# Layer 0's first weight product as seven block products, with every engine's order written out

## The chip, the cores and the metric

The kernel runs on one core of one Trainium2 chip. The metric is device time in microseconds (us), from the first to the last instruction of the core. The core has a matrix engine (PE; its weight loads are listed apart as PEld), a vector engine (DVE), an activation engine (ACT), a general engine (POOL, also called GpSimd) and a queue that only issues transfers (SP). [...]

## What is computed

Four graph layers run one after the other on x of 128 x 64 x 256 numbers (128 graphs, 64 nodes, 256 channels), all in fp32. The change touches only the first half of layer 0. Cut to what matters:

```python
h = jnp.maximum(_layernorm(x, axis=-1), 0.0)
x = x + _L0_gnn_ref(h, adj, W1, b1, g1, be1, W2, b2, g2, be2)

def _L0_gnn_ref(features, A, W1, b1, g1, be1, W2, b2, g2, be2):
    ...
    agg = jnp.einsum('nm,bmd->bnd', A_hat, features)
    x = agg.reshape(-1, d)
    h = jax.nn.relu(_batchnorm(x @ W1.T + b1, g1, be1))
    out = h @ W2.T + b2
    out = _batchnorm(out, g2, be2)
    return out.reshape(b, n, -1)
```

The batch norm takes its mean and variance over all 8192 rows (graphs times nodes). So no row of `h` can be made before the last row of `x @ W1.T` is there. Layer 1 (two graph products and four small LSTMs), layer 2 (attention) and layer 3 (attention with four heads) follow; they take about 1650 us of the time and are not touched.

## The kernel before

The 8192 rows are cut into 16 chunks of 512 rows (`CH = 512`, `NCH = 16`). A chunk is loaded as a tile of 128 partitions by 4 token tiles by 256 channels (`xt`, three buffers). Layer 0's first half does this for each chunk:

- `ln_stats` takes mean and variance of each token tile on DVE (`bn_stats`, line 159, and `bn_aggr`, line 160), then POOL computes one over the root (`rsqrt`, lines 99 and 100) and, in `ln_apply`, minus mean times that (lines 182 and 183). ACT applies both with a relu, one instruction for each of the four token tiles (line 187), which gives `h` (two buffers).
- `aggregate0` multiplies by the normalised adjacency, two graphs in one 128 x 128 block-diagonal matrix, and turns tokens by channels into channels by tokens on the way (`aggregate`, line 214). Each fp32 product counts as two instructions in the trace, so this is 64 small ones a chunk. The result lies in two PSUM banks; one is copied to the tile `agg` (two buffers) by DVE (line 354) and one by ACT (line 356).
- `product1` multiplies by W1: four blocks of 128 output channels, each over two blocks of 128 input channels, 512 columns wide (line 369; 16 instructions a chunk in the trace). ACT takes each block from PSUM and adds the bias b1 (line 371), and DVE takes its statistics for the batch norm (line 372). The results, `z1`, stay in SBUF for all 16 chunks: blocks 0 and 1 in a tile `z1a`, blocks 2 and 3 in a tile `z1b`.

After the last chunk `bn_params` makes scale and shift for each block of 128 channels from the statistics of all chunks (line 295 on DVE, 99 and 100 on POOL, 299 to 301 on DVE). `relu2` applies them to chunks 0 and 1 on ACT (line 376), and `product2` multiplies these two chunks by W2 (line 385), block by block as they come.

The second product of chunks 2 to 14 is made in another way already: the class `Seven2` takes the 2 x 2 blocks of a product and makes them with seven block products and sums of blocks (Winograd's form of Strassen's method). Its left sums of weights are `w2_sums` (line 508), its right sums are made by `differences` (lines 308 to 311), and its products (line 432) are 256 columns wide, 28 instructions a chunk. A PSUM bank named X collects products 1, 6, 7 and 4 one after the other and is read after each; Y collects 5 and 3; Z holds 2. The four right sums of a chunk lie in one tile of the tag `h1`, which has two buffers.

What sets the order: inside `manual_schedule(engines=...)` an engine named there takes its instructions in the order of the program; engines not named are ordered by a planner. Chunk 0 is written out for all engines, chunks 1 to 15 and `bn_params` for PE alone, `Seven2` for PE, DVE, ACT and POOL. Between these stretches stands `tc.no_sync_barrier()`, a boundary in the order of the instructions that makes no engine wait for another. [...]

## Time and profile before

| | |
|---|---|
| median of 3 runs | 1911.15 us (1910.53 to 1912.87) |
| span of the profiled execution | 1908.6 us |
| the same execution, as timed | 1910.73 us |
| PE busy | 1887.0 us of 1908.6 (99%) |
| DVE, ACT, POOL busy | 1190.7, 979.5, 444.6 us |
| layer 0's first half: chunk 2's aggregation to the first `product2` | 22.34 to 144.37 us |
| in these 122.03 us: PE, DVE, ACT, POOL busy | 121.72, 72.06, 74.65, 25.93 us |
| `Seven2`, steady part (182.49 to 230.80): PE, DVE, ACT, POOL busy of 48.31 us | 48.31, 42.89, 35.58, 39.07 us |

A line of the timeline gives the start and the length of a merged group in us, the engine, the line of the program, the operation, the tile written and read, shapes, and how many instructions were merged; in brackets stands how long the engine had been idle before and what released it. A group of PE instructions is longer than its share of the engine's time[...]: how fast PE goes is read from the distance between starts.

### The profile page before, as it was taken

Reading aid. Unit: us, or ns where it says so; the run is one execution under the profiler, and the core shown is the slowest. Engines: PE = TensorE matmul, PEld = TensorE weight load, DVE = VectorE, ACT = ScalarE, POOL = GpSimd, SP = SyncE. Lnnn points to the kernel's source line nnn. Section 1 sums busy time; section 2 is a strip of 40 time slices with the busy share of each in tenths; the row PEclk is TensorE's granted clock in tenths of the full one; section 3 lists DMA queues with packets and bytes.
Section 4 is the critical chain, followed back from the end, with each engine's and each line's share of the span. In section 5 each row is a group of like instructions: output and inputs, shape, how many; then the busy total and the mean of one; then the engine's idle time right before and its main releaser. Section 6 shows DMA issues by size and latency. Waiting matters only on the chain.

```text
span 1908.6 us, 38821 instructions
## 1 busy us (share of the span) xinstructions
PE 1887.0 (99%) x15137; PEld 1488.3 (78%) x15137; DVE 1190.7 (62%) x3070; ACT 979.5 (51%) x2184; POOL 444.6 (23%) x632
## 2 busy tenths in 40 slices
PE   8999999999999999999999999999999999999998
PEld 5446866886897898799689789879969967777776
DVE  6647844556557656655755764665555567777776
ACT  5657734455456455455544645545554544444453
POOL 4205711211211211121121121112112213232332
PEclk9999999999999999999999999999999999999999
DMA  4113653115424522531632452352144245444433
GB/s 137 60 39 138 223 195 108 49 78 188 132 84 161 182 84 77 189 103 70 215 117 84 161 182 84 103 186 100 54 155 127 92 133 156 134 150 139 144 112 112
DMA packets 110502, 240.39 MB, mean 126 GB/s; under 512 B 11376, under 2 KB 74352, under 8 KB 110320
## 3 DMA queue, kind: packets, MB, share of 16 engines
q1 hardware_dynamic: 109568, 236.57, 37.1%
q8 instruction: 120, 1.97, 0.4%
q0 software_dynamic: 320, 1.05, 0.2%
q14 instruction: 62, 0.51, 0.1%
q10 hardware_dynamic: 432, 0.30, 0.1%
HBM read 169.98 MB, written 67.90 MB: 125 GB/s over the span
## 4 chain that ended last, share of the span: by engine, by line
PE 93%; DVE 4%; ACT 1%; issue 1%; POOL 1%; DMA 0%; SPq 0%; DVEq 0%; ACTq 0%; POOLq 0%
PE x L990 23%; PE g L954 18%; PE z L990 11%; PE y L990 6%; PE v L1264 6%; PE z L369 5%; PE p_q L1271 3%; PE u L743 3%; PE v L729 3%; PE X L1460 3%; PE X L432 2%; PE Y L1460 1%; PE z L385 1%; PE Y L432 1%; PE agg_c L214 1%; PE o L1587 1%
## 5 line engine op out<-in xcount | busy, mean ns | idle before, releaser
L999 DVE TENSOR_TENSOR gates<-gates,x 128x128 f32<-128x128 f32 (+2 forms) x384 | 119.4, 322 | 333.1 <-PE x L990 327.7
L990 PE MATMUL x<-xd,wset 128*128 128x128 f32 (+2 forms) x1280 | 285.0, 310 | 0.1
L990 PE MATMUL x<-hd,wset 128*128 128x128 f32 (+2 forms) x1152 | 246.7, 303 | 0.0
L1048 POOL TENSOR_TENSOR gates<-gates 128x512 f32<-128x512 f32 (+2 forms) x48 | 75.0, 1562 | 647.9 <-ACT gates L882 647.9
L990 PEld LDWEIGHTS x<-xd,wset 128*128 128x128 f32 x1280 | 202.1, 190 | 16.9 <-DVE gates L999 3.1
L882 ACT ACTIVATE gates<-gates,bias 128x256 f32<-128x256 f32 (+4 forms) x384 | 170.4, 490 | 66.4 <-DVE gates L999 63.6
L990 PEld LDWEIGHTS x<-hd,wset 128*128 128x128 f32 x1152 | 185.1, 191 | 5.0
L933 ACT ACTIVATE gates<-g,bias 128x512 f32<-128x512 f32 (+2 forms) x240 | 138.2, 610 | 97.7 <-PE g L954 94.4
L954 PE MATMUL g<-hT,wset 128*128 128x256 f32 (+2 forms) x744 | 184.4, 405 | 1.1 <-DVE hT L893 1.1
L954 PEld LDWEIGHTS g<-hT,wset 128*128 128x128 f32 x744 | 140.5, 190 | 44.1 <-issue 8.8
L954 PE MATMUL g<-hT,wih 128*128 128x512 f32 x384 | 166.4, 592 | 0.0
L996 ACT COPY gates<-y 128x128 f32<-128x128 f32 (+2 forms) x192 | 54.2, 294 | 204.8 <-PE y L990 204.3
L990 PE MATMUL z<-hs,wset 128*128 128x128 f32 (+2 forms) x768 | 154.1, 303 | 0.0
L954 PEld LDWEIGHTS g<-hT,wih 128*128 128x128 f32 x384 | 72.3, 190 | 87.7 <-issue 83.0
L990 PEld LDWEIGHTS z<-hs,wset 128*128 128x128 f32 x768 | 119.8, 191 | 3.3
L369 PE MATMUL z<-agg,w_sb 128*128 128x512 f32 x256 | 114.1, 598 | 0.0
L939 DVE TENSOR_TENSOR cell<-gates 128x512 f32<-128x512 f32 (+2 forms) x80 | 50.5, 650 | 101.6 <-ACT gates L933 101.5
L999 DVE TENSOR_TENSOR gates<-gates,z 128x128 f32<-128x128 f32 (+2 forms) x384 | 104.6, 316 | 0.2
L996 ACT COPY gates<-x 128x128 f32<-128x128 f32 (+2 forms) x192 | 56.5, 296 | 93.7 <-PE x L990 93.0
L882 ACT ACTIVATE gates<-x,bias 128x128 f32<-128x128 f32 (+2 forms) x192 | 74.8, 390 | 50.9 <-PE x L990 48.1
L990 PE MATMUL z<-hT,wset 128*128 128x128 f32 (+1 forms) x512 | 96.9, 301 | 0.0
L369 PEld LDWEIGHTS z<-agg,w_sb 128*128 128x128 f32 x256 | 47.3, 190 | 54.6 <-issue 51.4
(271 smaller groups left out, 3827.0 us busy)
## 6 DMA issues: line engine op xcount, KB each, us to landing
wset<-wfar SPq DMA_DIRECT2D x96, 960.0 KB, 6.4
hT<-far_h SPq DMA_DIRECT2D x124, 128.0 KB, 2.9
far_h<-hm SPq DMA_DIRECT2D x16, 512.0 KB, 3.0
far_n<-xs SPq DMA_DIRECT2D x16, 512.0 KB, 6.9
xs<-far_n SPq DMA_DIRECT2D x64, 128.0 KB, 3.1
far_x<-xs SPq DMA_DIRECT2D x16, 512.0 KB, 3.0
x<-far_x SPq DMA_DIRECT2D x64, 128.0 KB, 3.2
xt<-in_x_dram SPq DMA_DIRECT2D x15, 512.0 KB, 4.0
```

The lines of the kernel that those rows point to most:

```text
L369: nc.tensor.matmul(ps, w1_sb[:, k, m * P : (m + 1) * P], agg[:, k, :], start=(k == 0), stop=(k == KD - 1))
L432: nc.tensor.matmul(self.banks[tag], w, right[:, k, :], start=first and not k, stop=True, skip_group_check=True)
L729: nc.tensor.matmul(banks[m], wg0_sb[:, k, m * P : (m + 1) * P], agg[:, k, :], start=(k == 0), stop=(k == KD - 1))
L882: nc.scalar.activation(gate(q, c, part), src, AF.Tanh if q == 2 else AF.Sigmoid, bias=bs[:, q * KD + c : q * KD + c + 1])
L933: nc.scalar.activation(columns_of(gate(q, c)), natural(banks[q, c][:, :n].rearrange("p (w b) -> p w b", b=nb)), AF.Tanh if q == 2 else AF. ...
L954: nc.tensor.matmul(banks[q, c][:, :n].rearrange("p (w b) -> p w b", b=nb)[:, w, :], block(q, c, k), hv[:, k, w.start * p : (w.stop - 1) * ...
L990: nc.tensor.matmul(folded(self.psum(kind)), wsets[p, self.q][:, BLOCKS[kind][i], :], (ox[self.s] if part == "x" else oh)[kind], start=firs ...
L996: nc.scalar.copy(gate(self.q, kind // 5, halves[kind // 5]), self.psum(kind))
L999: nc.vector.tensor_add(gate(self.q, *dst), gate(self.q, *a), self.psum(kind))
L1048: nc.gpsimd.tensor_mul(gates[:, 0, :, :n], gates[:, 0, :, :n], gates[:, 2, :, :n])
L1264: nc.tensor.matmul(ps[:, i, :], hT[:, k, j, :], w[:, k, first : first + D], start=(k == 0), stop=(k == KD - 1))
L1460: nc.tensor.matmul(st[c, tag][:, i * CH // 2 : (i + 1) * CH // 2].rearrange("p (a n) -> p a n", n=P), w, st[c, "o7"][kind], start=first an ...
```

## The change

Chunks 2 to 14 of `product1` become seven block products too, in a new class `Seven1`. The 2 x 2 blocks are the two 128-channel blocks of `agg` by its two halves of 256 columns. One product is two matrix products of 256 columns (four instructions in the trace), one for each 128 columns of the weight block. The left sums `w1_sums` are made by POOL from `w1_sb`; the four right sums of a chunk are made by POOL into a tile `t1` of tag `h1`. The same tile holds product 2 (`self.z`), which ACT copies out of PSUM and POOL adds to block (0, 0) (`c11`). Blocks are taken from PSUM by four ACT copies and two DVE additions per chunk. Chunks 0, 1 and 15 keep the plain product.

Chunks 1 to 15 are now written out in order for PE, DVE, ACT and POOL. In iteration `c` of the new loop stand the aggregation of chunk `c + 1` (both copies now on ACT), five products of chunk `c` and the last two of chunk `c - 1`, the right sums for `c + 1`, layer-norm statistics of chunk `c + 3`, and layer-norm application of chunk `c + 2`. Loads of x are issued for `c + 4`.

ACT copies `z1` without the bias; `bn_params` is called with `biased=False`, which adds b1 to the mean and then b1 times the scale to the shift, two small DVE instructions for each of the four blocks. `w2_sums` moves from the start of this stretch into iterations 7 to 10. `bn_params` for `bn1` and what follows are now behind a `no_sync_barrier()` of their own.

```diff
@@ -299,6 +300,9 @@
             nc.vector.tensor_mul(sc[:, one], sc[:, one], bn[:, 1, one])
             nc.vector.tensor_mul(sh[:, one], mv[:, m, 0:1], sc[:, one])
             nc.vector.tensor_sub(sh[:, one], bn[:, 2, one], sh[:, one])
+            if not biased:
+                nc.vector.scalar_tensor_tensor(sh[:, one], bn[:, 0, one], sc[:, one], sh[:, one],
+                                               op0=OP.mult, op1=OP.add)
         return sc, sh
...
@@ -336,41 +340,106 @@
     z1, z1whole, h1, hs, aggs = {}, {}, {}, {}, {}
+    xts, shifts = {}, {}
+    halves2 = [slice(0, CH // 2), slice(CH // 2, CH)]
     def load0(c):
-        xt = l0.tile([P, NJ, D], F32, tag="xt", name=f"xt_{c}", bufs=3)
-        nc.sync.dma_start(xt, xr[c])
-        hs[c] = l0.tile([P, NJ, D], F32, tag="h", name=f"h_{c}")
-        return xt
-    def norm0(c):
-        xt = load0(c)
-        ln_apply(hs[c], xt, *ln_stats(xt, f"a{c}"), f"a{c}", by_pool=True)
-    def aggregate0(c):
+        if c < NCH:
+            xts[c] = l0.tile([P, NJ, D], F32, tag="xt", name=f"xt_{c}", bufs=3)
+            nc.sync.dma_start(xts[c], xr[c])
+    def moments0(c):
+        return ln_moments(xts[c], f"a{c}", range(NJ)) if c < NCH else iter(())
+    def shift0(c, late):
+        for mv, rstd in late:
+            nmr = small.tile([P, NJ], F32, tag=f"ln_nmr{NJ}", name=f"nmr_a{c}")
+            nc.gpsimd.tensor_tensor(nmr, mv[:, :, 0], rstd, OP.mult)
+            nc.gpsimd.tensor_scalar(nmr, nmr, -1.0, None, op0=OP.mult)
+            shifts[c] = rstd, nmr
+    def apply0(c, *tiles):
+        if c >= NCH:
+            return
+        if c not in hs:
+            hs[c] = l0.tile([P, NJ, D], F32, tag="h", name=f"h_{c}")
+        rstd, nmr = shifts[c]
+        for j in tiles:
+            nc.scalar.activation(hs[c][:, j, :], xts[c][:, j, :], AF.Relu, bias=nmr[:, j : j + 1],
+                                 scale=rstd[:, j : j + 1])
+    def aggregate0(c, by_both=True):
         aggs[c] = l0.tile([P, KD, CH], F32, tag="agg", name=f"agg_{c}")
         dst = aggs[c].rearrange("p k (j e t) -> p e (k j) t", e=2, t=T)
         for e, ps in enumerate(aggregate(hs.pop(c), ahat_t, f"a{c}")):
-            if e == 0:
+            if by_both and e == 0:
                 nc.vector.tensor_copy(dst[:, e], ps)
             else:
                 nc.scalar.copy(dst[:, e], ps)
-    def product1(c):
-        agg = aggs.pop(c)
+    def new_z1(c):
         lo = res.tile([P, KD, CH], F32, tag=f"r{c}", name=f"z1a_{c}")
         hi = z1b.tile([P, KH - KD, CH], F32, tag=f"z{c}", name=f"z1b_{c}")
         z1[c] = [lo[:, m, :] for m in range(KD)] + [hi[:, m, :] for m in range(KH - KD)]
-        for m in range(KH):
-            if c == 0 and 2 * m == KH:
-                aggregate0(1)
-                ln_apply(hs[2], *third, "a2")
-            ps = bank(f"z1_{c}_{m}")
-            for k in range(KD):
-                nc.tensor.matmul(ps, w1_sb[:, k, m * P : (m + 1) * P], agg[:, k, :],
-                                 start=(k == 0), stop=(k == KD - 1))
-            nc.scalar.activation(z1[c][m], ps, AF.Identity, bias=bn1_sb[:, 0, m : m + 1])
+        z2[c], z1whole[c] = lo, (lo, hi)
+    def stats1(c, *ms):
+        for m in ms:
             nc.vector.bn_stats(st1[:, m, c, :], z1[c][m])
-        z2[c], z1whole[c] = lo, (lo, hi)
+    def block1(c, m, agg):
+        ps = bank(f"z1_{c}_{m}")
+        for k in range(KD):
+            nc.tensor.matmul(ps, w1_sb[:, k, m * P : (m + 1) * P], agg[:, k, :], start=(k == 0),
+                             stop=(k == KD - 1))
+        nc.scalar.copy(z1[c][m], ps)
+    class Seven1:
+        def __init__(self, c):
+            self.c, self.banks = c, {}
+            agg = aggs.pop(c)
+            b = {(k, j): agg[:, k, halves2[j]] for k in range(KD) for j in range(2)}
+            t = l0b.tile([P, KH, CH], F32, tag="h1", name=f"t1_{c}").rearrange("p k n -> p (k n)")
+            n = CH // 2
+            self.z = t[:, 4 * n : 6 * n]
+            t = [t[:, i * n : (i + 1) * n] for i in range(4)]
+            self.sums = differences(nc.gpsimd, t, b[0, 0], b[0, 1], b[1, 0], b[1, 1])
+            self.at = {1: b[0, 0], 2: b[1, 0], 3: b[1, 1], 4: t[3], 5: t[0], 6: t[1], 7: t[2]}
+        def product(self, kind, tag):
+            first = tag not in self.banks
+            if first:
+                self.banks[tag] = bank(f"{tag}1_{self.c}")
+            for i in range(2):
+                if kind in (1, 2, 4):
+                    m, k = {1: (0, 0), 2: (0, 1), 4: (1, 1)}[kind]
+                    w = w1_sb[:, k, (2 * m + i) * P : (2 * m + i + 1) * P]
+                else:
+                    w = w1_sums[:, {5: 0, 6: 1, 7: 2, 3: 3}[kind], i * P : (i + 1) * P]
+                nc.tensor.matmul(self.banks[tag][:, i * CH // 2 : (i + 1) * CH // 2], w, self.at[kind],
+                                 start=first and not i, stop=True, skip_group_check=True)
+        def part(self, m, j):
+            return z1whole[self.c][m][:, :, halves2[j]]
+        def ps(self, tag):
+            return self.banks[tag].rearrange("p (i n) -> p i n", i=2)
+        def copy(self, m, j, tag):
+            nc.scalar.copy(self.part(m, j), self.ps(tag))
+        def add(self, m, j, tag):
+            nc.vector.tensor_add(self.part(m, j), self.part(m, j), self.ps(tag))
+        def c11(self):
+            nc.gpsimd.tensor_tensor(self.part(0, 0), self.part(0, 0),
+                                    self.z.rearrange("p (i n) -> p i n", i=2), OP.add)
...
-        xt = load0(2)
-        third = xt, *ln_stats(xt, "a2")
-        product1(0)
+        load0(2)
+        third = ln_stats(xts[2], "a2")
+        agg = aggs.pop(0)
+        new_z1(0)
+        for m in range(KH):
+            if 2 * m == KH:
+                aggregate0(1)
+                hs[2] = l0.tile([P, NJ, D], F32, tag="h", name="h_2")
+                ln_apply(hs[2], xts[2], *third, "a2")
+            block1(0, m, agg)
+            stats1(0, m)
...
+        w1_sums = l0.tile([P, 4, D], F32, name="w1_sums", bufs=1)
         w2_sums = l0b.tile([P, 4, KH // 2, P], F32, name="w2_sums", bufs=1)
-        a = w2_sb.rearrange("p (i k) (m f) -> p i m k f", i=2, m=KD)
-        for dst, u, v, op in ((0, a[:, 0, 1], a[:, 1, 1], OP.add),
-                              (1, w2_sums[:, 0], a[:, 0, 0], OP.subtract),
-                              (2, a[:, 0, 0], a[:, 0, 1], OP.subtract),
-                              (3, a[:, 1, 0], w2_sums[:, 1], OP.subtract)):
-            nc.gpsimd.tensor_tensor(w2_sums[:, dst], u, v, op)
-        for c in range(1, NCH):
-            if c + 1 < NCH:
-                aggregate0(c + 1)
-            if c + 2 < NCH:
-                norm0(c + 2)
-            product1(c)
-        sc1, sh1 = bn_params(st1, bn1_sb, w0, "bn1", True)
+    tc.no_sync_barrier()
+    def sums_of(dst, a):
+        return [lambda d=d, u=u, v=v, op=op: nc.gpsimd.tensor_tensor(dst[:, d], u, v, op)
+                for d, u, v, op in ((0, a[:, 0, 1], a[:, 1, 1], OP.add),
+                                    (1, dst[:, 0], a[:, 0, 0], OP.subtract),
+                                    (2, a[:, 0, 0], a[:, 0, 1], OP.subtract),
+                                    (3, a[:, 1, 0], dst[:, 1], OP.subtract))]
+    with tc.manual_schedule(engines={mybir.EngineType.PE, mybir.EngineType.DVE,
+                                     mybir.EngineType.Activation, mybir.EngineType.Pool}):
+        load0(3)
+        load0(4)
+        aggregate0(2)
+        late = moments0(3)
+        for _ in range(NJ):
+            next(late)
+        shift0(3, late)
+        for f in sums_of(w1_sums, w1_sb.rearrange("p k (m f) -> p k m f", m=2)):
+            f()
+        late = moments0(4)
+        sevens = {2: Seven1(2)}
+        new_z1(1)
+        agg = aggs.pop(1)
+        load0(5)
+        for m in range(KH):
+            block1(1, m, agg)
+            next(late)
+            stats1(1, m)
+            if m:
+                apply0(3, *((0,), (1,), (2, 3))[m - 1])
+        for f in sevens[2].sums:
+            f()
+        shift0(4, late)
+        more = sums_of(w2_sums, w2_sb.rearrange("p (i k) (m f) -> p i m k f", i=2, m=KD))
+        for c in range(2, NCH - 1):
+            a, z = sevens[c], sevens.get(c - 1)
+            new_z1(c)
+            load0(c + 4)
+            aggregate0(c + 1, False)
+            b = sevens[c + 1] = Seven1(c + 1) if c + 1 < NCH - 1 else None
+            late = moments0(c + 3)
+            a.product(2, "Z")
+            nc.scalar.copy(a.z, a.banks["Z"])
+            next(late, None)
+            next(late, None)
+            apply0(c + 2, 0)
+            if z:
+                z.product(7, "X")
+                z.add(1, 1, "X")
+            if b:
+                for f in b.sums:
+                    f()
+            a.product(1, "X")
+            a.copy(0, 0, "X")
+            a.c11()
+            if z:
+                stats1(c - 1, 0, 1)
+            a.product(5, "Y")
+            a.copy(1, 1, "Y")
+            apply0(c + 2, 1)
+            next(late, None)
+            next(late, None)
+            if z:
+                z.product(4, "X")
+                z.copy(1, 0, "X")
+            apply0(c + 2, 2)
+            shift0(c + 3, late)
+            if c > 6 and more:
+                more.pop(0)()
+            if z:
+                stats1(c - 1, 2, 3)
+            a.product(6, "X")
+            a.copy(0, 1, "X")
+            apply0(c + 2, 3)
+            a.product(3, "Y")
+            a.add(0, 1, "Y")
+        c = NCH - 1
+        new_z1(c)
+        agg = aggs.pop(c)
+        for m in range(KH):
+            if not m:
+                a.product(7, "X")
+                a.add(1, 1, "X")
+                stats1(c - 1, 0, 1)
+            if m == 1:
+                a.product(4, "X")
+                a.copy(1, 0, "X")
+                stats1(c - 1, 2, 3)
+            block1(c, m, agg)
+            stats1(c, m)
+    tc.no_sync_barrier()
+    with tc.manual_schedule(engines={mybir.EngineType.PE}):
+        sc1, sh1 = bn_params(st1, bn1_sb, w0, "bn1", False)
         for c in range(2):
             new_h1(c)
         for k in range(KH):
```

More of the change, by code (lines that the diff above doesn't have):

```diff
@@ L446, in stats @@
             nc.vector.bn_stats(st2[:, m, self.c, :], z2[self.c][:, m, :])
-    halves2 = [slice(0, CH // 2), slice(CH // 2, CH)]
     with tc.manual_schedule(engines={mybir.EngineType.PE, mybir.EngineType.DVE,
@@ L458 @@
             nc.scalar.dma_start(adjt_bd[r, r], adj_t)
-        xts = [l0.tile([P, NJ, D], F32, tag="xt", name=f"xt_{c}", bufs=3) for c in range(2)]
+        for c in range(2):
+            xts[c] = l0.tile([P, NJ, D], F32, tag="xt", name=f"xt_{c}", bufs=3)
         nc.sync.dma_start(xts[0][:, : NJ // 2], xr[0][:, : NJ // 2])
```

## The prediction

> **What bounds the kernel now.** I read the busy shares first, then the windows of the stage that changes, then its timeline.
>
> ```profile
> PE 1887.0 (99%) x15137; PEld 1488.3 (78%) x15137; DVE 1190.7 (62%) x3070; ACT 979.5 (51%) x2184; POOL 444.6 (23%) x632
> ...
> 22.34:144.37 122.03, 121.72 (x1138) 59.25 (x1138) 72.06 (x189) 74.65 (x129) 25.93 (x59) 1.00 0.21 66
> ```
>
> PE has no idle time to speak of, here as elsewhere: between chunk 2's aggregation and the first second product it idles 0.3 of 122 us. So PE instructions removed count in full, and each wait that PE gets is a loss. The timeline gives the price of one chunk, before and in the form that `Seven2` already has:
>
> ```profile
> 47.88 1.16 PE L214 MATMUL agg_a<-ahat_t,h 64*64 64x64 f32 x64
> ...
> 48.97 7.13 PE L369 MATMUL z<-agg,w_sb 128*128 128x512 f32 x16
> ...
> 56.04 1.16 PE L214 MATMUL agg_a<-ahat_t,h 64*64 64x64 f32 x64
> ...
> 182.49 1.03 PE L432 MATMUL Z<-z1b,w_sb 128*128 128x256 f32 x4
> ...
> 188.53 1.03 PE L432 MATMUL Z<-z1b,w_sb 128*128 128x256 f32 x4
> ```
>
> From start to start a chunk takes 56.04 - 47.88 = 8.16 us: 1.09 for the aggregation, 16 x 0.429 = 6.86 for the product, 0.2 at the change between them. Twenty-eight instructions of 256 columns take 188.53 - 182.49 = 6.04 us, 0.863 for a product of four. Three more views bear on what the new order waits for.
>
> ```profile
> 25.17 1.41 POOL L508 TENSOR_TENSOR w_sums<-w_sb 128x256 f32<-128x256 f32 x2 [3.67 <-DMA w_sb<-in_w2t_dram]
> ...
> 28.13 0.23 POOL L99 TENSOR_SCALAR rstd_a<-mv_a 128x4 f32<-128x4 f32 x1
> ...
> 30.14 2.08 ACT L187 ACTIVATE h<-xt,nmr_a,rstd_a 128x256 f32<-128x256 f32 x4 [2.28 <-POOL nmr_a L183]
> ```
>
> POOL: four sums of 256 columns take 28.13 - 25.17 = 2.96 us, and from the start of the root to ACT's first use of the shift there are 2.01 us.
>
> ```profile
> 185.94 1.03 PE L432 MATMUL X<-t,w_sb 128*128 128x256 f32 x4
> ...
> 187.00 0.86 DVE L308 TENSOR_TENSOR t<-z1a 128x512 f32<-128x512 f32 x1 [0.75 <-PE X L432]
> ```
>
> The first right sum of a chunk, which overwrites a part of the tile that only product 5 has read, still waited for product 4 of the chunk before last, 1.06 us after that one's start. A buffer of `h1` comes free only whole.
>
> ```profile
> 23.01 1.29 DVE L372 BATCH_NORM_STATS2 st<-z1b 128x6 f32<-128x512 f32 x2 [2.76 <-ACT z1b L371]
> 24.22 0.27 DVE L144 TENSOR_SCALAR mask<-adj_bd 64x64 f32<-64x64 f32 x2
> ...
> 140.14 0.69 DVE L372 BATCH_NORM_STATS2 st<-z1a 128x6 f32<-128x512 f32 x1 [1.02 <-ACT z1a L371]
> 140.86 0.59 DVE L295 BATCH_NORM_AGGREGATE mv_bn<-st 128x2 f32<-128x96 f32 x1
> ...
> 143.05 1.52 ACT L376 ACTIVATE h<-z1a,sh_bn,sc_bn 128x512 f32<-128x512 f32 x2 [1.23 <-DVE sh_bn L301]
> 143.94 0.19 PEld L385 LDWEIGHTS z<-h,w_sb 128*128 128x128 f32 x1 [0.24 <-ACT h L376]
> ```
>
> Line 144 needs only `adj_bd`, there since 6 us, and DVE idled 2.76 us before line 372; yet it ran after it: nothing passes a `no_sync_barrier`. And today block 0's statistics (line 295) run while PE still multiplies blocks 1 to 3 of chunk 15; that hides the batch norm.
>
> [...] The first 34 `idle_a` transposes took 5.45 us, 33 steps of 0.157, where `idle_b` has steps of (1.47 - 0.27)/11 = 0.109: 1.6 us lost to a cold start. [...] here 128x512 takes 1.27 to 1.78 us on POOL (line 309) and 0.68 at best on DVE.
>
> **The change, part by part.**
>
> *Products.* For 13 chunks 16 x 0.429 = 6.86 becomes 6.04 us: 13 x 0.82 = -10.7 us, all on the path. Weight loads of 190 ns fit into steps of 216.
>
> *One iteration, if PE sets it:* 0.2 + 1.09 + 6.04 = 7.34 us. ACT: seven copies at a step of 0.49 (49.18 to 49.66 at line 356) and four applications at 0.49: 5.4 us. DVE: four tiles of statistics at 0.53, four statistics of 512 at 0.61, two additions at 0.6 (673 ns at line 772): 5.8 us. POOL: sums 2.96, `c11` 1.3 (line 309 at its quickest, 1.27), root and shift 2.0: 6.3 us; with one w2 sum (0.73) 7.0. All are below 7.34, so only order can hurt. ACT's order: a copy starts 1.12 us after its product's start (185.08 to 186.20). From product 5's start there follow 1.12, five ACT steps 2.46, the last application 0.59, the wait 0.06, the aggregation of that tile 0.4, products 2, 7 and 1 2.59: 7.2 us round, below 7.34. I take nothing; at 0.52 a step it would be 0.1 an iteration, +1.
>
> *The right sums' buffer.* `t1` of c + 1 takes the buffer of c - 1, so POOL waits for product 4 of c - 1, in the middle of iteration c. From its start: 1.1, sums 2.96, `c11` 1.3, root and shift 2.0, which reach ACT in iteration c + 1, there application 0.49, copy of block (0, 0) 0.59, 0.09 to PE, where product 6 waits to write into that bank: 8.55 us. PE comes to product 6 after 7.34 + 0.86 = 8.20. So 0.35 us are lost, and after such a loss the next round starts later and meets none: every second iteration, 5 times (4 to 12), +1.8 us. Contention is the unknown: at line 580's mean of 858 ns and line 309's slow 1.78 the chain is 0.99 longer. Those rows ran beside DVE operations with two SBUF inputs; the new stage has none on DVE, so I take the lower value.
>
> *Start.* Iteration 2 needs the shift of chunk 4, in POOL's queue behind chunk 3's shift (done at 30.0), w1's sums (33.0) and the right sums of 2 (36.0): done at 38.0. Chunk 3's shift also holds ACT: application 30.0, block 2's copy, application, block 3's copy, two applications to 33.1, aggregation done at 33.4, where the kernel before began its product at 32.66: +0.8. Then product 2 to 34.3, 1 to 35.2, 5 to 36.05; product 6 waits for ACT's copy, behind the application at 38.05: 38.05 + 0.49 + 0.59 + 0.09 = 39.2: +3.2. Behind that ACT instruction are all copies; they catch up within two products. The next shift (POOL: 3.0 + 1.3 + 2.0 after 38.0, at 44.4) is in time.
>
> *End.* `bn_params` now stands behind a boundary, and DVE before it in the order of the program. After the last matmul step of block 3: copy at +0.31, 0.62 later its statistics, +0.72 line 295, then 2.19 to ACT's relu (140.86 to 143.05) and 0.19 for the added shift instruction (the added mean runs under POOL's root), 0.89 to the weight load, 0.1: 5.0 us in which PE has nothing; before, there was no gap. +5.0. Later blocks come every 2.5 us and PE needs one every 3.4.
>
> *Half clock.* [...] 0 to +1.6; I take 0.5.
>
> *At nothing:* ACT's copies without bias are shorter than those with it (585 for 680 ns) and beside PE; the second aggregation copy on ACT is counted above; w2's sums leave POOL's queue at 25.17, where chunk 3's shift waited behind them only until 28.13, when its statistics would be just done anyway; x loads (4.0 us to land) are released by the last application of c + 1 and needed an iteration later; SP's other issues here (line 531 at 117.6) wait for buffers, not for the order of x loads. Chunk 0's part stays behind PE.
>
> Sum: -10.7 + 1.8 + 0.8 + 3.2 + 5.0 + 0.5 = +0.6 us. Against its own span: 1908.6 to 1909.2. That execution was timed at 1910.73, between the lowest and the median run, so the sum goes on the median: 1911.15 + 0.6 = 1911.7 us. What a measurement of this kernel can tell from no change is about 0.2%, 3.8 us.
>
> **Rivals.**
>
> *Forecast, the saving is eaten by waits: 1911.7* (1908 to 1915), chance 0.52.
>
> *B, one of the two edge waits is not there.* If the planner gets block 0's parameters ahead of DVE's last statistics, or POOL's queue reaches chunk 4's shift by 35, 3 to 5 us come back: 1911.7 - 5.0 = 1906.7. For it: POOL is idle from 21.5 to 27.8 and could take w1's sums there, were the order not written. Against it: line 144. Chance 0.22.
>
> *C, POOL becomes the bound, slower.* Place: the chain from product 4 through sums, `c11`, root and shift to product 6. Price: with 0.86 a sum and 1.78 for `c11` it is 9.54, 1.34 lost every second iteration: 6.7 for 1.8, and the start's eight sums cost 1.0 more: +5.9, 1917.6. It decides from 4.3 us for four sums and `c11` together. For it: 7 of the 13 rows of line 309 in `Seven2`'s stage took 1.78, and POOL is the engine with the least room. Against it: 0.72 to 0.73 at line 508 beside the same DVE statistics. Chance 0.26.
>
> *That it doesn't do what it says* would need seven products to take PE as long as eight; the 6.04 us exclude it.
>
> **How the numbers follow.** The forecast gives 0.02 faster, 0.46 same, 0.04 slower; B 0.18 faster, 0.04 same; C 0.04 same, 0.22 slower: 0.20, 0.54, 0.26. The range goes to 1905.5 (B with half clock absent and a little of the start back) and 1918 (C): outside lie some 0.06 of B, 0.07 of C and 0.03 of the rest.
>
> **What would show it.** Right: iterations of 7.3 to 7.7 us between aggregations; product 6 of chunk 2 released by ACT some 3 us late, ACT by POOL's shift; first right sum starting 1.1 us after product 4; a PE gap of 5 us before line 385. Wrong: aggregations 8 us apart, right sums starting straight after the aggregation's copies, no gap at the end, or PE at half clock within the loop.

## The result and the profile after

| | before | changed |
|---|---|---|
| median, first chip | 1911.54 us (4 runs) | 1918.43 us (4 runs, 1918.02 to 1920.37) |
| ratio | | 1.0038 (95% interval 1.0020 to 1.0055) |
| median, second comparison (e10 below) | 1911.88 us | 1917.84 us; ratio 1.0034 (1.0022 to 1.0047) |
| span of the profiled execution | 1908.6 us | 1916.4 us |
| chunk 2's aggregation to the first product of `Seven2` | 135.76 us | 141.85 us |

The change makes the kernel slower, by 6 to 7 us. The forecast was 1911.7 us, no change, with a range up to 1918.0: the first median lies 0.4 us beyond the range, that of the second comparison just inside it.

Where the 7.8 us between the spans lie: the last row of the table holds 6.1 of them. The start up to chunk 2's aggregation is 0.5 shorter. `Seven2`'s steady part is the same in both (81.82 and 81.83 us from its first product to the last chunk's second product). Another 1.9 lie between there and layer 1's first large product; e10 and e11 below show that one kernel's executions differ by as much there. Some 0.3 remain behind it. Two lines of the kernel before, the aggregation of chunk 4 and the first product of `Seven2`, from which stretches are measured below:

```profile
39.72 1.16 PE L214 MATMUL agg_a<-ahat_t,h 64*64 64x64 f32 x64
...
158.10 1.03 PE L432 MATMUL Z<-z1b,w_sb 128*128 128x256 f32 x4
```

Busy shares of the changed kernel's page, then its row of windows for chunk 2's aggregation to the first second product (columns: stretch, length, busy us and instructions of PE, weight loads, DVE, ACT and POOL, granted clock, DMA share, GB/s):

```profile
PE 1885.9 (98%) x15293; PEld 1522.4 (79%) x15293; DVE 1203.0 (63%) x3091; ACT 984.8 (51%) x2210; POOL 499.0 (26%) x701
...
21.87:148.32 126.45, 115.50 (x1293) 89.62 (x1293) 86.49 (x219) 80.88 (x157) 83.04 (x132) 0.97 0.23 72
```

Before, PE idled 0.3 of 122 us here; now it idles 11 of 126, and its clock is no longer whole (0.97). Three places hold it.

*The loop.* Timeline of the changed kernel, two iterations:

```profile
49.35 1.16 PE L214 MATMUL agg_a<-ahat_t,h 64*64 64x64 f32 x64
...
54.00 1.03 PE L425 MATMUL X<-t,w_sb 128*128 128x256 f32 x4
54.08 0.60 ACT L369 ACTIVATE h<-xt,nmr_a,rstd_a 128x256 f32<-128x256 f32 x1 [1.82 <-POOL nmr_a L359]
...
55.29 1.10 PE L425 MATMUL X<-t,w_sums 128*128 128x256 f32 x4 [0.26 <-ACT z1a L435]
...
57.00 0.58 ACT L435 COPY z1a<-X 128x512 f32<-128x512 f32 x1
57.19 1.41 PE L214 MATMUL agg_a<-ahat_t,h 64*64 64x64 f32 x64
57.46 0.62 ACT L369 ACTIVATE h<-xt,nmr_a,rstd_a 128x256 f32<-128x256 f32 x1
58.52 1.13 PE L425 MATMUL Z<-agg,w_sb 128*128 128x256 f32 x4
...
62.08 1.03 PE L425 MATMUL X<-t,w_sb 128*128 128x256 f32 x4
...
63.26 0.72 POOL L312 TENSOR_TENSOR t<-agg 128x256 f32<-128x256 f32 x1 [1.90 <-PE X L425]
...
64.77 1.16 PE L214 MATMUL agg_a<-ahat_t,h 64*64 64x64 f32 x64
```

Iterations take 57.19 - 49.35 = 7.84 and 64.77 - 57.19 = 7.58 us by turns, where PE alone would take 7.34. In the first, ACT gets chunk 6's shift from POOL late (54.08) and product 6 comes 55.29 - 54.00 - 0.86 = 0.43 late. That lateness runs on along ACT: the last application of the next chunk (57.46) reaches the aggregation late too, which then takes 58.52 - 57.19 = 1.33 us up to the next product instead of 1.09. The row at 63.26 is the cause: POOL's first right sum waits for product 4 and starts 1.18 us after it.

*The start.* Timeline, then windows of one microsecond (the last number but two is the clock):

```profile
37.01 0.24 POOL L359 TENSOR_SCALAR nmr_a<-nmr_a 128x4 f32<-128x4 f32 x1
...
37.29 0.60 ACT L369 ACTIVATE h<-xt,nmr_a,rstd_a 128x256 f32<-128x256 f32 x1 [2.54 <-POOL nmr_a L359]
37.79 0.57 ACT L435 COPY z1a<-X 128x512 f32<-128x512 f32 x1
...
38.50 1.71 PE L425 MATMUL X<-t,w_sums 128*128 128x256 f32 x4 [2.66 <-ACT z1a L435]
...
40.00 1.91 PE L425 MATMUL Y<-agg,w_sums 128*128 128x256 f32 x4
```

```profile
38.00:39.00 1.00, 0.50 (x2) 0.50 (x3) 0.00 (x0) 1.00 (x3) 1.00 (x2) 0.93 0.00 0
...
40.00:41.00 1.00, 1.00 (x4) 0.82 (x3) 0.00 (x0) 0.75 (x2) 1.00 (x2) 0.50 0.00 0
...
42.00:43.00 1.00, 1.00 (x64) 1.00 (x64) 0.97 (x2) 0.00 (x0) 0.92 (x2) 0.86 0.15 23
```

Product 6 of chunk 2 waits 2.66 us for ACT's copy of product 1 (37.79), which stands behind an application (37.29), which waits for POOL's shift (37.01); in e2 below, where that shift comes at 34.70, the copy runs at 35.68. Then the clock is at half from about 38.9 to 42.3 (0.50 in each window between 39 and 42), after PE has begun again at 38.50: products 6 and 3 take 41.85 - 38.50 = 3.35 us up to the next aggregation instead of 1.9.

*The end.* Timeline:

```profile
137.13 5.31 PE L395 MATMUL z<-agg,w_sb 128*128 128x512 f32 x12
...
143.71 1.01 DVE L296 BATCH_NORM_AGGREGATE mv_bn<-st 128x2 f32<-128x96 f32 x2
...
144.66 0.58 DVE L296 BATCH_NORM_AGGREGATE mv_bn<-st 128x2 f32<-128x96 f32 x1
...
147.15 0.34 DVE L304 SCALAR_TENSOR_TENSOR sh_bn<-bn_sb,sc_bn,sh_bn 128x1 f32<-128x1 f32 x2
...
147.46 2.92 ACT L445 ACTIVATE h<-z1a,sh_bn,sc_bn 128x512 f32<-128x512 f32 x4 [4.39 <-DVE sh_bn L304]
...
148.32 2.08 PE L454 MATMUL z<-h,w_sb 128*128 128x512 f32 x2 [5.88 <-ACT h L445]
...
163.72 1.03 PE L501 MATMUL Z<-z1b,w_sb 128*128 128x256 f32 x4
```

A step is one PE instruction of 512 columns, 0.429 us from start to start. The first product's last step ends at 142.27 (twelve steps from 137.13), so the gap is 6.05 us. `bn_params` takes 147.46 - 143.71 = 3.75 us to the first relu: DVE takes three blocks' parameters side by side, where the kernel before made block 0's alone in 2.19 us. The second product of chunks 0 and 1 then takes 163.72 - 148.32 = 15.40 us to the first product of `Seven2` where it took 13.73: half clock again, from 144.67 to 151.50 (0.84 in the window 144 to 145, 0.50 in each up to 151, 0.75 in 151 to 152).

The half clock is not a matter of the one profiled execution: the granted clock was 0.996 or 0.997 in all nine executions of the changed kernel (four here, five in e10), and 0.998 to 1.000 in all those of the kernel before that the experiments below are compared with.

### The profile page after: what moved, and what is told of

Its sections match the earlier page's. It is cut to its first block, busy times and chain, and to the rows that moved or that the text cites. A ratio compares the mean times of both kernels' runs of the same rounds, so it can differ in the third digit from the quotient of the medians.

```text
span 1916.4 us, 39280 instructions
## 1 busy us (share of the span) xinstructions
PE 1885.9 (98%) x15293; PEld 1522.4 (79%) x15293; DVE 1203.0 (63%) x3091; ACT 984.8 (51%) x2210; POOL 499.0 (26%) x701
## 3 DMA queue, kind: packets, MB, share of 16 engines
q0 software_dynamic: 320, 1.05, 0.2%
## 4 chain that ended last, share of the span: by engine, by line
PE 90%; DVE 4%; POOL 3%; ACT 1%; issue 1%; DMA 0%; SPq 0%; DVEq 0%; POOLq 0%; ACTq 0%
PE x L1151 23%; PE g L1115 18%; PE z L1151 11%; PE y L1151 6%; PE v L1425 5%; PE p_q L1432 3%; PE u L904 3%; PE v L890 3%; PE X L1621 3%; PE X L501 2%; PE X L425 2%; PE Y L1621 1%; PE Y L501 1%; PE agg_c L214 1%; PE o L1748 1%
## 5 line engine op out<-in xcount | busy, mean ns | idle before, releaser
L1151 PE MATMUL x<-hs,wset 128*128 128x128 f32 (+2 forms) x384 | 84.8, 303 | 0.0
L1220 ACT ACTIVATE gates<-cell 128x256 f32<-128x256 f32 (+2 forms) x144 | 55.3, 384 | 51.2 <-DVE cell L1219 51.1
```

The costliest lines, as they stand in the source:

```text
L1151: nc.tensor.matmul(folded(self.psum(kind)), wsets[p, self.q][:, BLOCKS[kind][i], :], (ox[self.s] if part == "x" else oh)[kind], start=firs ...
```

## The experiments

My theory: the seven products do save 0.82 us a chunk, and the waits that the new order makes, with the half clock behind them, use it up. Three of them can be taken out alone: the end, w1's sums at the start, the right sums' buffer. A stage time below is from the start of chunk 2's aggregation to the first product of `Seven2` in the run's trace: before 135.76, changed 141.85. Medians come with the median of the kernel before on the same chip.

**e1: batch norm's parameters and relus in the hand-written block.**

```diff
             block1(c, m, agg)
+            if m == 1:
+                relu2(0, 0)
+                relu2(1, 0)
             stats1(c, m)
+            if not m:
...
+                sc1, sh1 = bn_params(st1, bn1_sb, w0, "bn1", False, blocks)
...
+            if m < 2:
+                blocks[0](m)
...
     tc.no_sync_barrier()
...
-        sc1, sh1 = bn_params(st1, bn1_sb, w0, "bn1", False)
```

> The changed kernel, with the parameters of layer 0's second batch norm and its eight ReLUs taken out of the piece of program behind the boundary and written by hand into the block of chunk 15: parameters of block 0 behind the statistics of block 0, parameters of block 1 and ReLUs of block 0 behind block 1, the rest behind. Output unchanged. My theory (the boundary makes every engine begin the parameters only after the last block product, [...]): the gap of 6.05 us before the second product falls to at most 1 us and the 1.7 us of half clock after it go too, so 6.5 to 7.5 us faster than the changed kernel, about 1911 us. Rival 1 (the gap is hidden by the work behind it, DVE or DMA bound there): the gap goes in the trace and the time moves by less than 2 us. Rival 2 (the tail was slow because the engines compute there as fast as they can, boundary or not): the gap stays above 4 us and nothing is gained.

Measured: 1909.97 us against 1912.3, ratio 0.9988 (0.9980 to 0.9996); stage 132.58. Timeline of e1, start and end, and one window of the start:

```profile
39.59 1.10 PE L430 MATMUL X<-t,w_sums 128*128 128x256 f32 x4 [2.66 <-ACT z1a L440]
...
136.64 5.31 PE L400 MATMUL z<-agg,w_sb 128*128 128x512 f32 x12
...
137.32 0.59 DVE L296 BATCH_NORM_AGGREGATE mv_bn<-st 128x2 f32<-128x96 f32 x1
...
139.83 1.52 ACT L450 ACTIVATE h<-z1a,sh_bn,sc_bn 128x512 f32<-128x512 f32 x2 [0.69 <-DVE sh_bn L304]
...
141.79 13.90 PE L459 MATMUL z<-h,w_sb 128*128 128x512 f32 x32
```

```profile
39.00:40.00 1.00, 0.41 (x2) 0.41 (x3) 0.00 (x0) 1.00 (x3) 1.00 (x3) 1.00 0.00 0
```

The parameters of block 0 are made while PE still multiplies blocks 1 to 3, alone and in 139.83 - 137.32 = 2.51 us; the gap is gone (141.79 is twelve steps after 136.64), and so is the half clock behind it (155.52 - 141.79 = 13.73 us). That alone makes the kernel faster than before, by 0.04 to 0.20%. The stage gained 9.3 us and not the 7.7 of gap and clock: nearly all of the rest, 1.4 us, is at the start, where nothing was changed. There product 6 waits the same 2.66 us, but the clock stays whole. Whether that gap costs half clock thus differs between executions.

**e2: the sums of w1 earlier on POOL.**

```diff
         w2_sums = l0b.tile([P, 4, KH // 2, P], F32, name="w2_sums", bufs=1)
...
+        for f in sums_of(w1_sums, w1_sb.rearrange("p k (m f) -> p k m f", m=2)):
+            f()
     tc.no_sync_barrier()
...
         shift0(3, late)
-        for f in sums_of(w1_sums, w1_sb.rearrange("p k (m f) -> p k m f", m=2)):
-            f()
         late = moments0(4)
```

> The changed kernel, with the four sums of w1's blocks issued on POOL at the end of the second piece of the program instead of between the shifts of chunks 3 and 4. Output unchanged. My theory (product 6 of chunk 2 stood 2.66 us because POOL's queue held the sums ahead of the shift of chunk 4, and the gap halved PE's clock for 3.4 us): the stall falls under 0.5 us, the half clock between 39 and 42.5 us goes, 3 to 4.5 us faster than the changed kernel, about 1914.5 us. Rival 1 (POOL is simply too slow in this stretch; the sums are only elsewhere in its way): the stall comes back at another instruction within chunks 2 to 4 and less than 1 us is gained. Rival 2 (only the stall counts, the half clock is not its consequence): about 2.5 us are gained and the half clock stays.

Measured: 1915.39 against 1912.3, ratio 1.0017 (1.0010 to 1.0025); stage 138.44. Timeline of e2:

```profile
35.18 0.60 ACT L369 ACTIVATE h<-xt,nmr_a,rstd_a 128x256 f32<-128x256 f32 x1
35.36 1.03 PE L425 MATMUL Y<-t,w_sums 128*128 128x256 f32 x4
...
36.40 1.10 PE L425 MATMUL X<-t,w_sums 128*128 128x256 f32 x4
```

ACT's application no longer waits, and product 6 comes 36.40 - 35.36 = 1.04 us after product 5. Chunk 2's aggregation to chunk 4's takes 16.01 us instead of 19.98: 2.5 us of wait and 1.4 of half clock. No other instruction took over the stall, so POOL was not too slow here, only its queue in the wrong order.

**e3: right sums in three buffers of their own.**

```diff
-            t = l0b.tile([P, KH, CH], F32, tag="h1", name=f"t1_{c}").rearrange("p k n -> p (k n)")
+            t = l0t.tile([P, 3 * CH], F32, tag="t1", name=f"t1_{c}")
...
+        l0t, close_l0t = pool("l0t", 3, "right")
```

The buffers are closed behind the loop, and the tiles of tag `h1` open in a pool of their own there, two as before.

> The changed kernel, with the right sums in a pool of their own of three buffers instead of sharing the two of h1 (the pool closes and h1's opens behind the loop). Output unchanged. My theory (in every second iteration product 6 waits for POOL, which began its chain behind product 4 of the chunk before because of the two buffers, and the aggregation behind it waits for the last application for the same reason): both stalls go, iterations are all 7.34 to 7.45 us instead of 7.58 and 7.82, 3 to 4 us faster than the changed kernel over 12 iterations, about 1915 us. Rival 1 (POOL's or ACT's own work per iteration is the limit): the period stays at about 7.6 or above and the first right sum waits for something else (the copies of the aggregation); under 1 us is gained. Rival 2 (only the .43 of product 6 goes, not the application's .24): periods 7.5, about 2 us gained.

Measured: 1916.04 against 1912.3, ratio 1.0017 (1.0009 to 1.0026); stage 139.56. Timeline of e3:

```profile
49.06 1.16 PE L214 MATMUL agg_a<-ahat_t,h 64*64 64x64 f32 x64
...
51.48 0.73 POOL L312 TENSOR_TENSOR t<-agg 128x256 f32<-128x256 f32 x1 [1.15 <-ACT agg L379]
...
56.39 1.16 PE L214 MATMUL agg_a<-ahat_t,h 64*64 64x64 f32 x64
...
144.34 17.08 PE L454 MATMUL z<-h,w_sb 128*128 128x512 f32 x32 [5.88 <-ACT h L445]
```

Every iteration now takes 7.33 us. The first right sum starts when its aggregation has been copied, and nothing is late behind it. From chunk 4's aggregation to the last twelve steps of the first product it is 91.42 us instead of 95.28: 3.9 us. POOL's and ACT's own work, unchanged, is therefore not the limit. The stage gained only 2.3 of these 3.9, because in this execution half clock took 3.2 us from the second product (161.26 - 144.34 = 16.92) and not 1.7.

**e4: the three edits together.**

> The three edits together: parameters and ReLUs in the hand-written order, the sums of w1's blocks early, right sums in three buffers. Output unchanged. My theory (the seven products save 10 to 11 us of PE time and the waits of the new order eat it): 13 to 15.5 us faster than the changed kernel, 1903 to 1905.5 us, so about 7 us faster than the kernel before. Rival 1 (the waits overlap one another's causes, so that taking one away moves the next one in): less than 9 us, about 1910 or slower. Rival 2 (some of the loss lies downstream, where the bias of layer 1 came late, and depends on what comes before): up to 2 us more or less than the sum of the three single edits.

Measured: 1903.74 us (1902.83 to 1906.26) against 1912.3, ratio 0.9958 (0.9944 to 0.9972). The stage is 126.34 us, 15.5 below the changed kernel's; the three single edits gained 9.3 + 3.4 + 2.3 = 15.0. The row of windows of e4 from chunk 2's aggregation to the second product:

```profile
22.14:134.74 112.60, 111.35 (x1293) 88.74 (x1293) 83.26 (x204) 81.29 (x156) 80.66 (x126) 1.00 0.22 72
```

PE idles 1.25 of 112.6 us, at whole clock. The edits add up and don't hide each other. That the two sums agree to 0.5 us is partly luck, since each trace lost another amount to half clock (1.4 us at the start of the changed kernel, none in e1; 1.7 us at its end, 3.2 in e3); without half clock the changed kernel's stage would be 138.8 us, and e4's is 12.4 below that, where the buffer, w1's sums and the gap are 3.9 + 2.5 + 6.05 = 12.45. This version is 8.6 us faster than the kernel before and the best of the study.

**e5: the boundary alone, in the kernel before.**

```diff
             product1(c)
+    tc.no_sync_barrier()
+    with tc.manual_schedule(engines={mybir.EngineType.PE}):
         sc1, sh1 = bn_params(st1, bn1_sb, w0, "bn1", True)
```

> The kernel before, with nothing changed but a boundary without barrier between the last chunk's product and the parameters of the second batch norm. Output unchanged. My theory (the boundary alone opens the gap ahead of the second product, whatever products stand before it): the gap grows from 0.3 us to 5 to 6 us and PE's clock is halved in and after it, so 5.5 to 8 us slower than the kernel before, about 1918 us. Rival (the gap comes from the hand-written block, which ends with late statistics): the gap stays under 2 us and the time is within 2 us of before.

Measured: 1920.92 against 1911.91, ratio 1.0045 (1.0033 to 1.0057); stage 143.59. Timeline of e5:

```profile
145.70 1.46 DVE L295 BATCH_NORM_AGGREGATE mv_bn<-st 128x2 f32<-128x96 f32 x3
...
149.27 2.93 ACT L376 ACTIVATE h<-z1a,sh_bn,sc_bn 128x512 f32<-128x512 f32 x4 [4.22 <-DVE sh_bn L301]
...
150.14 2.07 PE L385 MATMUL z<-h,w_sb 128*128 128x512 f32 x2 [5.81 <-ACT h L376]
```

The boundary makes the gap of 6 us and the half clock (15.58 us for the second product, 13.73 before; its first two instructions take 2.07 us, and 2.08 in the changed kernel, where the clock was 0.50), with plain products ahead of it and none of the hand order; the second new line only takes up PE's order again. Here too three blocks' parameters run side by side: 3.57 us to the relu, where it was 2.19 with block 0 alone. The median rose by 9.0 us, more than the 5.5 to 8 expected; the stage of the profiled execution, the quickest of the five, accounts for 7.8.

**e6: filling the gap with transposes.**

```diff
         sc1, sh1 = bn_params(st1, bn1_sb, w0, "bn1", False)
+        keep_busy(52, "t")
```

> The changed kernel, with 52 additional transposes of the identity on PE between the last block product and the second product; their result is not read, output unchanged. My theory (the half clock behind the gap is a cost of its own): the second product begins at the same distance from the last block product (6.0 to 6.3 us) but takes 13.7 instead of 15.4 us, so 1.2 to 3 us faster than the changed kernel, about 1916.5 us. Rival (the clock falls for another reason than idleness, or the transposes hold the second product up): no gain, or slower by up to 1 us.

Measured: 1915.74 against 1911.91, ratio 1.0021 (1.0014 to 1.0028). Timeline of e6:

```profile
142.66 5.84 PE L151 MATMUL idle_t<-ident 128*128 128x128 f32 x52
148.72 14.00 PE L454 MATMUL z<-h,w_sb 128*128 128x512 f32 x32 [0.22 <-ACT h L445]
```

The second product begins as late as before (11.21 us after the start of the last twelve steps; 11.19 in the changed kernel) and takes 13.84 us. The ratio is 0.0013 to 0.0017 below the changed kernel's two, some 3 us, though the intervals of the ratios overlap. The profiled execution does not stand for the total: it took 1921.49 us, by far the longest of the 17, with a late load for layer 1 behind this stage. The granted clock of all 17 speaks for the trace's reading: 0.998 in the middle and 0.997 at the lowest, where the changed kernel had 0.996 or 0.997 (0.001 less is 3.8 us more at half clock, worked out from a span of 1916). So the half clock is a loss of its own behind the gap, and work without use removed it: the clock was 1.00 from 142.2 to 156, and the second product took 13.84 us for 15.40.

**e7: only the bias in the shift.**

```diff
-            nc.scalar.activation(z1[c][m], ps, AF.Identity, bias=bn1_sb[:, 0, m : m + 1])
+            nc.scalar.copy(z1[c][m], ps)
...
-        sc1, sh1 = bn_params(st1, bn1_sb, w0, "bn1", True)
+        sc1, sh1 = bn_params(st1, bn1_sb, w0, "bn1", False)
```

> The kernel before, with the bias of the first product added by the batch norm's shift (a plain copy on ACT where an activation with bias stood, one DVE instruction more for each block of parameters). Output unchanged. My theory: this part of the change costs nothing that can be measured, within 1 us of the kernel before (four DVE instructions more on the way to the second product, of about 0.1 us each, one of them on the path). Rival (part of the 1.9 us lost further down, where layer 1's bias comes late, belongs to this part): about 2 us slower, with a wait of DVE for that bias above 2 us as in the changed kernel; in the kernel before it was 0.4 us.

Measured: 1912.01 against 1911.91, ratio 1.0002 (0.9993 to 1.0010); stage 135.65. This part costs nothing that can be measured: at most 0.1%, 1.9 us.

**e8 and e9: the hand order with plain products.**

```diff
-            a, z = sevens[c], sevens.get(c - 1)
...
+            agg = aggs.pop(c)
+            for m in range(KH):
+                block1(c, m, agg)
+                stats1(c, m)
...
+                apply0(c + 2, m)
```

> The changed kernel with its order by hand, its boundaries and its bias in the shift, but chunks 2 to 14 again by plain products of four blocks (no sums of w1, no right sums, no block products in layer 0; layer 1's and the second product's remain). Output unchanged. My theory (the products save 0.82 us a chunk, 10.7 us in 13; the right sums cost 3.8 us in the loop and 4 us at the start, which go here): iterations of 8.16 us, no stall at the start, the gap of about 6 us before the second product stays; 10.7 - 7.8 = 3 us slower than the changed kernel, 1920 to 1923 us, so 8 to 11 us slower than before. Rival 1 (the order by hand is what cost, for ACT now makes all the copies): iterations above 8.3 us, 1925 us or more. Rival 2 (the products save less than their count says): at or below the changed kernel, 1918 us or faster.

Measured: 1929.33 against 1911.91, ratio 1.0092 (1.0079 to 1.0105), as rival 1 had it and not my theory. Timeline of e8:

```profile
57.75 0.93 PE L214 MATMUL agg_a<-ahat_t,h 64*64 64x64 f32 x48
...
58.99 0.46 PE L214 MATMUL agg_a<-ahat_t,h 64*64 64x64 f32 x16 [0.31 <-ACT h L369]
```

But it was my own order of this kernel, not the one of the change: the fourth tile's application stood last on ACT, the aggregation was cut in two, and an iteration took 8.70 us. With the applications moved forward (e9):

```diff
-                apply0(c + 2, m)
+                apply0(c + 2, *((0, 1), (2,), (3,), ())[m])
```

> As the last kernel (order by hand, boundaries and bias in the shift, but plain products in chunks 2 to 14), with one thing mended: there the last tile's application of the normalization stood in ACT's order behind the copy of the fourth block, so that each aggregation waited for it and an iteration took 8.70 us; here two applications follow the first block's copy and one each the next two. Output unchanged. My theory: iterations of 8.16 us as in the kernel before, the gap of 6 us before the second product and its half clock stay; 13 times 0.54 = 7 us faster than the last kernel, 1921 to 1923.5 us, so 9 to 11 us slower than before and 2.5 to 5 us slower than the changed kernel. Rival (the order by hand costs in the loop by itself): iterations above 8.3 us, 1925 us or more.

Measured: 1923.82 against 1911.88, ratio 1.0059 (1.0045 to 1.0073); stage 146.19; iterations of 8.155 us, as in the kernel before. The time lies 0.3 us above the 1921 to 1923.5 expected. The order by hand costs nothing in the loop; it costs at its two ends. From the kernel before (135.76) the stage grew by 10.4 us: 0.8 where chunk 3's aggregation waits tile by tile for ACT, 1.7 behind it, where PE goes at half speed (weight loads 0.85 us apart from 33.90 to 36.46, 0.43 from 37.06 on), 6.0 of gap and 1.95 at the end, where the second product takes 15.68 us for 13.73. Against e9 the seven products gain 146.19 - 141.85 = 4.3 us of the 10.7 that they save.

**e10 and e11: both kernels again.**

> The changed kernel once more, unaltered, beside the others on one chip, with a second trace. Question: is the wait of DVE for layer 1's bias (2.62 us in the first trace of the changed kernel, 0.41 in that of the kernel before; 1.9 us on the path) a part of the change or of the single execution? If of the change: the second product's end to the first large product of layer 1 takes again 22 to 23 us and before's again 20.7. If of the execution: both vary by 1 us or more between traces of one kernel. Time by my theory 1918 to 1920 us.

> The kernel before once more, unaltered, for a second trace: if the late bias belongs to the execution, the stretch from the last second product to layer 1's first large product is 21 us or more in it; if it belongs to the change, it is 20.7 us again.

Measured: e10 1917.84 against 1911.88, ratio 1.0034 (1.0022 to 1.0047), stage 141.68; e11 stage 135.75, one run of 1912.16. What released DVE ahead of layer 1's bias addition (the bias tile's view, us and times), in e11 and then in e10:

```profile
  DMA bias<-in_bhh_dram: 2.1, 1
```

```profile
  DMA bias<-in_bhh_dram: 2.3, 1
```

In the first traces it was 0.4 before and 2.6 changed. From the last second product to layer 1's first large product the two traces of the kernel before took 20.67 and 22.42 us, those of the changed kernel 22.59 and 22.61 (to the second aggregation in layer 1: 28.38 and 30.63, 30.30 and 30.71). The late bias comes in both kernels, and one execution of the kernel before differs from another by as much as the 1.9 us between the first two spans. So these 1.9 us can't be put down to the change. That no part of them belongs to it isn't shown either: the wait was 0.4, 0.6, 1.6 and 2.1 us in the four traces without the order by hand (before, e5, e7, e11) and 2.2 to 4.3 us in the nine with it. Why the load lands later in most executions stays open.

## Why the prediction was wrong

| step | predicted | measured | from |
|---|---|---|---|
| products | -10.7 | -10.7 | iterations of 8.155 (before, e9) and 7.33 us (e3), 13 chunks |
| right sums' buffer | +1.8 | +3.9 | e3 |
| start | +4.0 | +3.7 | traces of e1 and e10, without half clock |
| end | +5.0 | +6.05 | gap in the changed kernel |
| half clock | +0.5 | +3.1 | 1.4 at the start, 1.7 behind the gap; 0 and 3.2 in e10 |
| sum | +0.6 | +6.05 | stage: +6.09 |

The mechanism was the right one, and each wait stood where it had been placed: "the saving is eaten by waits". The sum failed in the sizes of three terms.

*Half clock*, the largest, is mis-sized by 2.6 us. The step "0 to +1.6; I take 0.5" priced one gap. It put the start, whose wait of 3.2 us it had worked out two steps earlier, at nothing without a reason; and its upper bound of 1.6 was an estimate of mine, the time that `idle_a` lost in the trace before, at a recorded clock of 1.00 throughout, where the end gaps brought 6.8 us at a clock of 0.50 (changed, e2, e3, e10). Seven traces with an end gap of about 6 us lost 1.7 to 3.2 us in the second product, 2.4 in the mean, and none of them lost nothing. With 2.4 for the end alone the forecast would have been 1913.6.

*The right sums' buffer* is mis-sized by 2.1 (1.8 predicted, 3.9 in e3). The chain of 8.55 us and its 0.35 in every second iteration were nearly right (0.43). What the step left out is that the last application stands on ACT behind the copy of product 6 (57.00 and 57.46 in the timeline): a late product 6 makes the next aggregation late as well, and each of the other iterations loses its 0.24.

*The end* is mis-sized by 1.05 (5.0 predicted, 6.05 measured). The step took 2.19 us from DVE's statistics to the relu out of the trace before, where block 0 came alone. Behind the boundary the statistics of all blocks are there before block 0's parameters begin, three blocks run side by side, and block 0 takes 3.75; alone and in the order by hand it took 2.51 in e1. *The start* was right to 0.3 us. From chunk 2's aggregation to chunk 4's there would be 17.38 - 2.55 = 14.83 us without a wait (the stretch before, with five products of 0.863 for sixteen steps of 0.429); e1 and e10 took 18.55 and 18.51, where no half clock fell on PE's work after the wait, and e2 16.01. So w1's sums cost 2.5 (predicted 3.2) and chunk 3's aggregation with the rest 1.2 (predicted 0.8).

Rival C ended near the measured time, but its cause fell. POOL ran at its low durations: in the loop, four right sums and `c11` took 4.14 us from 55.18, below the 4.3 from which that rival would decide, and in e3 the same POOL work held nothing up. The prediction's ground for the low durations was weaker than it looks: in the trace before, the quick rows of line 309 (1.27 to 1.28 us) ran beside a DVE operation with two SBUF inputs too (line 310), the slow ones (1.78) beside two (lines 310 and 311). That rival's number came near by luck. Rival B didn't come by itself; e1 and e2 are what it describes, made by hand.

Of the signs named, product 6 of chunk 2 behind ACT and POOL's shift, the first right sum 1.2 us after product 4, and the gap ahead of the second product were there. Of the iterations, by turns 7.58 and 7.84 us, only every second one lay in the 7.3 to 7.7 given. One sign of being wrong came as well: PE at half clock within the loop, in its first iteration (38.9 to 42.3).

## What to carry to other kernels

When PE has no idle time, price a change by writing down for each new wait both the time PE stands and what the clock takes afterwards: here the waits and their clock cost 17 us against a saving of 10.7. An order written by hand is won or lost at its ends: work that the planner had slipped across a stage's edge (the batch norm's parameters, weight sums into an idle POOL) has to be put there by hand as well. Where a buffer comes free in the middle of the next round, one buffer more can be worth as much as a third of the saving (here 3.9 of 10.7 us).

## What the runs showed of the hardware

A gap of PE of 2.66 to 2.68 us at the start brought 3.4 us at a clock of 0.50 in the changed kernel (from 38.9 to 42.3), in e3 (37.9 to 41.3) and in e6 (38.9 to 42.3), beginning between 0.4 us before and 0.4 after PE had started again; in e1 the same gap brought none (1.00 in every window from 32 to 45). What decides between them isn't shown. In e9 and e10 PE went at half speed even behind chunk 3's aggregation, where the longest gap was 0.51 us, twice: in e9 by the steps of its weight loads (0.85 us up to 36.46), in e10 by the clock (0.50 from 35 to 36, 0.55 from 36 to 37). The same two gaps brought none in the changed kernel's first trace, in e1, e2 and e3, where product 2 behind them took 0.96 to 0.97 us up to the next product; in e10 it took 1.52. In e10 that cost nothing, because PE had to wait for product 6 anyway: it came 16.62 us after chunk 2's aggregation began, 16.63 in the changed kernel's first trace. How much idle time it takes isn't shown.

At the end gaps of about 6 us the clock stood at half for 6.8 us in the changed kernel (144.67 to 151.50), e2 (142.4 to 149.2), e3 (143.7 to 150.6) and e10 (146.1 to 153.0), and fell between 2.4 and 5.5 us after PE's last product. What it cost depended on how much of it lay behind the gap: 1.7 us where it fell 3.6 us before the second product (changed), 3.2 where it fell 0.6 before (e3 and e10). In e5, e8 and e9, behind gaps as long (5.8 us of idle PE, 5.9 in the other four), the second product took 1.85, 2.4 and 1.95 us longer than its 13.73.
